# Attention weights as one exponential of a difference of logarithms, and a part of their sums as exact f32r products in three passes, in a four-layer graph network kernel

## The chip, the cores and the metric

The kernel runs on one core of a Trainium2 chip. The time is that of one execution on the device, in microseconds (us), and lower is better. Three runs of the kernel before took 836.5, 840.3 and 846.0 us. A core has several engines that run side by side, each with a queue of its own: TensorE (PE, matmuls; PEld are its weight loads), VectorE (DVE), ScalarE (ACT), GpSimd (POOL) and SyncE (SP, which issues most of the large loads).

## The reference

Four residual layers run one after the other on x (2708 nodes, 128 features) with one adjacency matrix adj (2708 x 2708). Each is followed by a layernorm. The change touches only the second, an attention layer:

```python
XW = jnp.matmul(X, W)
s_col = jnp.matmul(XW, a[0, :f])
s_row = jnp.matmul(XW, a[0, f:])
Z1 = jax.nn.leaky_relu(s_row[:, None] + s_col[None, :], negative_slope=0.01)
den = jnp.exp(Z1)
num = jnp.matmul(A, den)
att = jnp.where(num != 0, den / jnp.where(num != 0, num, 1.0), 0.0)
H = jnp.matmul(A, jnp.matmul(att, XW))
...
x = _layernorm(x + _L1_gnn_ref(x, adj, L1_gnn_W, L1_gnn_a), axis=-1)
```

Since exp(leaky(z)) is exp(0.01 z) times max(exp(0.99 z), 1), and z is a sum of a row's and a column's term, the factors exp(0.01 s) can be taken out of the large products. What stays for every pair of nodes is max(exp(0.99 (r + s)), 1), divided by num.

## The kernel before

The whole kernel is one program for one core. Most of it works on tiles of 128 partitions with up to 512 columns[...] ("psum" tiles with the tags acc0 to acc5 and twice ps). First comes layer 0 (matmuls L928), with row sums and degrees beside it. Then the nodes are sorted by one of their attention terms into GM = 24 groups of up to 126 nodes (lines 1324 to 1533). Then `grouped_attention` (line 1564) does the attention layer up to att @ XW, and `fast_rest` the rest of layer 1 and the layers 2 and 3 (the matmuls L1952, L1820, L2444, L2460).

`grouped_attention` goes over the 2708 columns in two halves of HALF = 1354, and in each over the 24 groups, so that q counts 48 groups. A half's columns are cut into chunks of 512, 512 and 330. For each q:

- `gather(q)` (L1577, on POOL) fetches the group's 126 adjacency rows from HBM three groups ahead into one of four places `gat[q]`; the first two rows of a place are free. `group_xw` (L1587) fetches the group's rows of XW.
- `numerators(q)` (line 1610) first writes max(q_b * gj_l, 1) for the group into `att` (L1618, DVE), where `q_b` and `gj_l` hold the exponentials of 0.99 times the two terms. Then for each chunk: a matmul (L1629, PE) of the group's 128 x 128 matrix with the gathered rows into a PSUM tile `num`; a copy of two rows of `num` into the first two rows of the next group's place (L1632, DVE), which carries running sums from group to group; the logarithm of `num` (L1634, ACT) into `ln_n`. Then, in the first half, the matrix of the group three ahead is made (`group_matrix`, L748, ACT; its spread of factors by a transpose on PE, L745, lies in the third chunk's tile). Last comes exp(-ln_n) over all 1354 columns (L1648, ACT). `num` tiles take turns in five buffers (`num_tags`).
- `weighted(q - 1)` (line 1650) multiplies `att` by it (L1652, DVE).
- `aggregate(q - 2)` (line 1654) adds XW's rows of the group times `att` to three sums `uacc`, one for each chunk (L1660, PE). At a half's end the sums are copied to `ut` (L1672 on ACT, L1675 on DVE).

The loop over q (line 1696) writes these out in this order, one group after the other. `queued(engine)` fixes that an engine issues the instructions within it in the order in which they are written. Beside the groups, the loop places small work: transposes of the first half's result (`node_major_u`, L1596 on PE, L1599 on ACT, in "ps" buffers) in groups 27 to 36, `tail_factors` (line 1679) at group 26, with a copy `repeated(x, ...)` (L218, DVE) in it, `added_up` (line 1550, DVE) at group 36, and `checked` (line 1559) at group 38. After the loop the remaining twelve transposes follow, among the first matmuls of the next stage.

An f32 matmul of up to 512 columns appears as two passes in the trace, with a weight load each. `sharp_products` (line 1816) in the later stages computes the same kind of product otherwise: both factors are cut into an upper part, a low part and a mix that are exact in the f32r format, and three f32r passes follow, two into a sum "upper" and one into the common sum. The two are joined at the end by a multiplication with 1 + 1/4096 and an addition. `split_rows` (line 1802) cuts the moving factor: one operation on ACT (L1806) and two on DVE (L1807, L1808).

Of the kernel before, what the change touches and what calls it, by code (L numbers as in the profile page):

```python
# [10 lines left out]
F32 = mybir.dt.float32  # L11
# [25 lines left out]
FIRST = 3  # L37
GM = 24
# [25 lines left out]


# [20 lines left out]
def kernel(  # L86
# [1225 lines left out]
    with ctx_keep:  # L1312
# [11 lines left out]
        with tc.tile_pool(name="sort", bufs=1) as st_p:  # L1324
# [54 lines left out]
            for b in range(NB):  # L1379
                w, cs = width(b), bslice(b)  # L1380
                sum_rows((3,3,2,2,1,1)[b])
                with queued(PE):
                    pr = bcast_block(rcl[:, 0, :], b, f"rb{b}")
                with queued(ACT):
                    nc.scalar.activation(q_b[:, cs], pr[:, :w], AF.Exp, scale=0.99)
# [137 lines left out]
            nc.vector.tensor_scalar(bi, e2_l, unit0[:, 1:2], None, op0=ALU.add)  # L1523
            nc.vector.tensor_copy(w_first[:, :, 0], sc[:, :FIRST])
# [39 lines left out]
    def grouped_attention(u_sb, rows_g):  # L1564
        adj_h = adjT.rearrange("k (h w) -> (k h) w", h=2)
        chunks = [(0, BW), (BW, 2 * BW), (2 * BW, HALF)]
        with tc.tile_pool(name="main", bufs=1) as mp:
            w_all = mp.tile([P, GM, P], F32, tag="w_all", name="w_all")
            xw_g = mp.tile([P, GM, F], F32, tag="xw_g", name="xw_g")
            gat, att, ln_n, uacc = {}, {}, {}, {}  # L1570
            num_tags = [("acc3", 1), ("acc4", 1), ("acc5", 1), ("ps", 2), ("ps", 2)]
# [38 lines left out]
            def numerators(q):  # L1610
# [6 lines left out]
                with queued(DVE):  # L1617
                    nc.vector.tensor_scalar(  # L1618
                        att[q], q_b[:, h0 : h0 + HALF], gj_l[:, g : g + 1], 1.0, op0=ALU.mult, op1=ALU.max
                    )  # L1620
                w = (w_first if g < FIRST else w_all)[:, g, :]
                for c, (ca, cb) in enumerate(chunks):
                    tag, nb = num_tags[(3 * q + c) % 5]
                    num = psum.tile([P, BW], F32, tag=tag, name=f"num{q}_{c}", bufs=nb)
                    if c == 2 and 0 < q and q + FIRST < GM:
                        with queued(PE):
                            group_spread_out(num[:, BW - P :], q + FIRST)
                    with queued(PE):
                        nc.tensor.matmul(num[:, : cb - ca], lhsT=w, rhs=gat[q][:, ca:cb], start=True, stop=True)  # L1629
                    if g + 1 < GM:  # L1630
                        with queued(DVE):
                            nc.vector.tensor_copy(gat[q + 1][0:2, ca:cb], num[0:2, : cb - ca])  # L1632
                    with queued(ACT):
                        nc.scalar.activation(  # L1634
                            ln_n[q][:, ca:cb],
                            num[:, : cb - ca],
                            AF.Ln,
                            scale=occ_l[:, g : g + 1],
                            bias=inval[:, g : g + 1],
                        )  # L1640
                if g + 1 == GM and not h:
                    carry(q + 1)
                if q + FIRST < GM:
                    pg = gb[:, FIRST, :] if q == 0 else num[:, BW - P :]
                    with queued(ACT):
                        group_matrix(w_all, q + FIRST, pg)
                with queued(ACT):
                    nc.scalar.activation(ln_n[q], ln_n[q], AF.Exp, scale=-1.0)  # L1648

            def weighted(q):  # L1650
                with queued(DVE):
                    nc.vector.tensor_mul(att[q], att[q], ln_n[q])  # L1652

            def aggregate(q):
# [3 lines left out]
                for c, (ca, cb) in enumerate(chunks):  # L1658
                    with queued(PE):
# [5 lines left out]
                            stop=(g == GM - 1),  # L1665
                        )
                if g == GM - 1:
                    for c, (ca, cb) in enumerate(chunks):
                        src, dst = uacc[h][c][:, : cb - ca], ut[:, h * HALF + ca : h * HALF + cb]
                        if c < 2:  # L1670
                            with queued(ACT):
                                nc.scalar.copy(dst, src)  # L1672
                        else:
# [5 lines left out]
            def tail_factors():  # L1679

                pt = ps_tile("tail_ps")
                repeated(x, NF * P)
# [13 lines left out]
            for q in range(2 * GM + 2):  # L1696
# [12 lines left out]
                if q == GM + GM // 4:  # L1709
                    with tc.issue_after(behind):  # L1710
                        fit_nodes()
                if q == GM + 2:
# [5 lines left out]
                if q == GM + GM // 2 + 2:  # L1718
# [899 lines left out]
```

## Time and profile before

| | |
|---|---|
| median of three runs | 840.3 us |
| lowest and highest | 836.5 and 846.0 us |
| the profiled execution | 836.5 us, its span 834.8 us |
| layer 0 and the row sums | 46 to 176 us of the span, PE busy 126.7 us |
| sorting into groups | 176 to 228 us, PE busy 47.9 us |
| attention, first half | 228 to 343 us, PE busy 114.4, DVE 101.9, ACT 91.6, POOL 94.7 us |
| attention, second half | 344 to 443 us, PE busy 99.0, DVE 89.2, ACT 75.2, POOL 57.5 us |
| layers 1 (rest), 2 and 3 | 457 to 835 us |

The costliest groups of the attention loop, as the page has them (line, engine, operation, output and inputs, shape, count, then busy us and mean ns of one, idle time of the engine before them and what ended it):

```profile
L1634 ACT ACTIVATE ln<-num,inval,occ_l 128x512 f32<-128x512 f32 x144 | 98.3, 725 | 46.5 <-DVE rows_g L1632 42.8
L1660 PE MATMUL uacc<-att,xw_g 128*128 128x512 f32 (+1 forms) x288 | 116.7, 542 | 0.3 <-PE num L1629 0.3
L1629 PE MATMUL num<-rows_g,w_all 128*128 128x512 f32 (+1 forms) x252 | 105.0, 543 | 0.2 <-issue 0.2
L1648 ACT ACTIVATE ln<-ln 128x1354 f32<-128x1354 f32 x48 | 64.1, 1336 | 0.9
```

How to read it: "<-" before a name of an engine says what released the waiting engine. The busy time of matmuls is modelled and their ends overlap, so PE's cadence is better read from the starts of the weight loads. A difference of 0.3 us of idle time in front of 288 matmuls says that nearly nothing is waited for there.

### The profile page before, as it was taken

What the parts mean: (1) busy time and instruction counts of PE and PEld (TensorE: products, weight loads), DVE (VectorE), ACT (ScalarE), POOL (GpSimd) and SP (SyncE); (2) the same over time, 40 slices, a digit from 0 to 9 for tenths busy, and PEclk for the clock granted to TensorE, in tenths of its full rate; (3) what the DMA queues carried; (4) which work ended last, traced back from release to release, by engine and by line L of the source; (5) the groups of instructions that cost most, each with busy time, mean ns of one, the idle gap of its engine ahead of it and who ended that gap; (6) DMA issues with size and microseconds to landing.
All of it is one profiled execution on the core that took longest, in us unless ns stands there. A gap on an engine that the chain in (4) does not pass through costs nothing.

```text
span 834.8 us, 10277 instructions
## 1 busy us (share of the span) xinstructions
PE 796.1 (95%) x3372; PEld 444.4 (53%) x3372; DVE 619.8 (74%) x1400; ACT 498.5 (60%) x887; POOL 194.9 (23%) x173
## 2 busy tenths in 40 slices
PE   4789999998999999999999999999999999999995
PEld 3345454454344555444454455564455766677774
DVE  4787645589598888889996677897588863776774
ACT  4856544214397878777776243686455665666662
POOL 5231000001388887576641000000000000000000
PEclk9799999999999999999999999999999999999997
DMA  9997559089479555445435778795985752756600
GB/s 341 366 383 274 143 34 372 28 307 382 157 258 393 179 165 172 134 121 179 150 117 176 270 266 284 238 345 190 360 288 160 239 179 69 290 188 239 226 27 16
DMA packets 94985, 181.70 MB, mean 218 GB/s; under 512 B 6272, under 2 KB 37396, under 8 KB 94584
## 3 DMA queue, kind: packets, MB, share of 16 engines
q1 hardware_dynamic: 85228, 142.62, 50.1%
q0 software_dynamic: 7680, 34.85, 13.1%
q10 hardware_dynamic: 2016, 3.49, 1.1%
q8 instruction: 29, 0.48, 0.2%
q14 instruction: 32, 0.26, 0.1%
HBM read 176.68 MB, written 4.28 MB: 217 GB/s over the span
## 4 chain that ended last, share of the span: by engine, by line
PE 83%; DVE 8%; DMA 5%; ACT 2%; issue 1%; ACTq 0%; DVEq 0%
PE a L1952 17%; PE uacc L1660 13%; PE num L1629 12%; PE a L928 11%; PE a L2460 7%; PE a L2444 6%; PE a_u L1820 5%; DMA A<-in_adjT_dram 4%; PE a L1820 2%; PE t L866 2%; DVE jk L1392 2%; PE pp L2347 1%; PE su L290 1%; PE xw L1063 1%; PE mx L2136 0%
## 5 line engine op out<-in xcount | busy, mean ns | idle before, releaser
L1634 ACT ACTIVATE ln<-num,inval,occ_l 128x512 f32<-128x512 f32 x144 | 98.3, 725 | 46.5 <-DVE rows_g L1632 42.8
L1660 PE MATMUL uacc<-att,xw_g 128*128 128x512 f32 (+1 forms) x288 | 116.7, 542 | 0.3 <-PE num L1629 0.3
L928 PE MATMUL a<-A,q_b 128*128 128x512 f32 (+2 forms) x264 | 110.8, 569 | 3.8 <-DVE q_b L963 2.6
L1577 POOL DMA_INDIRECT rows_g<-in_adjT_dram,row_i x48 | 97.3, 2028 | 62.5 <-PE num L1629 29.7
L1629 PE MATMUL num<-rows_g,w_all 128*128 128x512 f32 (+1 forms) x252 | 105.0, 543 | 0.2 <-issue 0.2
L2444 PE MATMUL a<-mask,node 128*128 128x452 f32 (+1 forms) x252 | 94.8, 458 | 0.0
L1632 DVE COPY rows_g<-num 2x512 f32<-2x512 f32 x138 | 81.2, 612 | 11.7 <-PE num L1629 7.6
L1952 PE MATMUL a<-cb,q_b 128*128 128x512 f32 (+1 forms) x222 | 89.5, 540 | 0.0
L1660 PEld LDWEIGHTS uacc<-att,xw_g 128*128 128x128 f32 x288 | 54.5, 190 | 55.1 <-issue 46.4
L2427 ACT ACTIVATE mask<-cb 128x904 fp32r<-128x904 f32 (+2 forms) x66 | 60.8, 923 | 35.0 <-PE a L2444 31.6
L1952 PE MATMUL a<-cb,xw 128*128 128x512 f32 (+1 forms) x196 | 79.4, 532 | 0.0
L1652 DVE TENSOR_TENSOR att<-att,ln 128x1354 f32<-128x1354 f32 x48 | 74.4, 1549 | 2.5 <-ACT ln L1648 2.5
L928 PEld LDWEIGHTS a<-A,q_b 128*128 128x128 f32 (+1 forms) x264 | 47.1, 196 | 53.9 <-issue 48.4
L1629 PEld LDWEIGHTS num<-rows_g,w_all 128*128 128x128 f32 x252 | 45.3, 190 | 44.8 <-issue 35.0
L2460 PE MATMUL a<-cb,edge 128*128 128x452 f32 (+1 forms) x150 | 68.9, 543 | 0.0
L1648 ACT ACTIVATE ln<-ln 128x1354 f32<-128x1354 f32 x48 | 64.1, 1336 | 0.9
L2444 PEld LDWEIGHTS a<-mask,node 128*128 128x128 f32 x252 | 46.2, 189 | 26.5 <-issue 24.1
L1219 ACT ACTIVATE xw<-A 128x2048 f32<-128x2048 f32 (+3 forms) x36 | 57.0, 1583 | 2.7 <-DMA A<-in_adjT_dram 1.8
L1587 POOL DMA_INDIRECT xw_g<-xw_d,xw_i x24 | 54.2, 2259 | 15.9 <-issue 15.6
L1952 PEld LDWEIGHTS a<-cb,q_b 128*128 128x128 f32 x222 | 38.4, 190 | 31.5 <-issue 29.4
L1618 DVE TENSOR_SCALAR att<-q_b,gj_l 128x1354 f32<-128x1354 f32 x48 | 44.4, 926 | 10.9 <-PE uacc L1660 10.9
L1806 ACT ACTIVATE a_s<-cb 128x512 fp32r<-128x512 f32 x43 | 26.6, 626 | 40.3 <-PE a L1820 29.5
(536 smaller groups left out, 1255.1 us busy)
## 6 DMA issues: line engine op xcount, KB each, us to landing
cb<-in_adjT_dram SPq DMA_DIRECT2D x10, 2816.0 KB
A<-in_adjT_dram SPq DMA_DIRECT2D x25, 1024.0 KB
cb<-in_adjT_dram SPq DMA_DIRECT2D x10, 2560.0 KB
B<-in_adjT_dram SPq DMA_DIRECT2D x18, 1024.0 KB
cb<-in_adjT_dram SPq DMA_DIRECT2D x5, 2486.0 KB
cb<-in_adjT_dram SPq DMA_DIRECT2D x5, 2260.0 KB
cb<-in_adjT_dram SPq DMA_DIRECT2D x2, 1554.0 KB
cb<-in_adjT_dram SPq DMA_DIRECT2D x1, 2464.0 KB
```

The source lines that it names most:

```text
L928: nc.tensor.matmul(acc[c][:, :w], lhsT=z[:kw, k, :], rhs=t[:kw, i, :w], start=c not in begun, stop=(d == NB - 1 and k == NT - 1), skip_gro ...
L1577: got = nc.gpsimd.indirect_dma_start(out=gat[q], out_offset=None, in_=adj_h, in_offset=bass.IndirectOffsetOnAxis(ap=row_i[:, h, g : g + 1] ...
L1629: nc.tensor.matmul(num[:, : cb - ca], lhsT=w, rhs=gat[q][:, ca:cb], start=True, stop=True)
L1632: nc.vector.tensor_copy(gat[q + 1][0:2, ca:cb], num[0:2, : cb - ca])
L1634: nc.scalar.activation(ln_n[q][:, ca:cb], num[:, : cb - ca], AF.Ln, scale=occ_l[:, g : g + 1], bias=inval[:, g : g + 1],)
L1648: nc.scalar.activation(ln_n[q], ln_n[q], AF.Exp, scale=-1.0)
L1652: nc.vector.tensor_mul(att[q], att[q], ln_n[q])
L1660: nc.tensor.matmul(uacc[h][c][:, : cb - ca], lhsT=xw_g[:, g, :], rhs=att[q][:, ca:cb], start=(g == 0), stop=(g == GM - 1),)
L1952: nc.tensor.matmul(acc()[:, :w], lhsT=weights[:, k, :], rhs=a, start=(k == 0), stop=False, skip_group_check=True)
L2427: nc.scalar.activation(mask[:, :n, :w], hold[i][0][:, t : t + n, :w], AF.Sign)
L2444: nc.tensor.matmul(acc()[:, :w], lhsT=node[:, k, j, :], rhs=mask, start=(k == 0 and j == 0 and b != 1), stop=False, skip_group_check=True,)
L2460: nc.tensor.matmul(acc()[:, :w], lhsT=edge[:, k, :], rhs=piece(k), start=(k == 0 and b == 1), stop=False, skip_group_check=True,)
```

## The change

- **One exponential.** `q_b` now holds 0.99 times the row term itself (a Copy on ACT in place of an Exp, L1385). `e1_l` and `e2_l`, once used, are filled with +0.99 and -0.99 times the group's terms. The multiplication and maximum of L1618 and the product L1652 go, and so does the exponential L1648. In their place `exponents(q)` computes max(q_b, e2_l) - ln_n in one DVE operation over 1354 columns, and `weighted(q)` takes Exp of it with the bias e1_l on ACT.
- **Order.** From the third group on (EARLY = 2), the copy of the two carried rows stands behind the chunk's logarithm instead of before it. `group_matrix` stands directly behind the third logarithm. The Exp of group q - 1 stands behind the logarithms of group q. `aggregate` takes the chunks in the order 1, 2, 0.
- **Three passes.** In the groups 3, 5, ..., 21 of each half, the first chunk (512 columns) is summed in three f32r passes, two into a new sum `upper` and one into `uacc`. `split_xw` cuts XW's rows of the group (128 columns: one operation on ACT, three on DVE), and `weighted` cuts the weights (512 columns: one on ACT, two on DVE). `upper` takes the PSUM bank acc5, so that the numerators share four buffers from the fourth group on. At a half's end one DVE operation joins `upper` to the copied sum.
- **Small work.** `repeated(x, ...)` moves from group 26 to group 24, `checked` from group 38 to group 40.

```diff
-                    nc.scalar.activation(q_b[:, cs], pr[:, :w], AF.Exp, scale=0.99)
+                    nc.scalar.activation(q_b[:, cs], pr[:, :w], AF.Copy, scale=0.99)
...
+            nc.vector.tensor_scalar(e1_l, value, 0.99, None, op0=ALU.mult)
+            nc.vector.tensor_scalar(e2_l, value, -0.99, None, op0=ALU.mult)
...
+SPLIT = (range(3,GM-2,2), range(3,GM-2,2))
...
+            first_tags = [("acc3", 1), ("acc4", 1), ("acc5", 1), ("ps", 2), ("ps", 2)]
+            num_tags = [("acc3", 1), ("acc4", 1), ("ps", 2), ("ps", 2)]
...
-                with queued(DVE):
-                    nc.vector.tensor_scalar(
-                        att[q], q_b[:, h0 : h0 + HALF], gj_l[:, g : g + 1], 1.0, op0=ALU.mult, op1=ALU.max
-                    )
...
-                    if g + 1 < GM:
+                    if q < EARLY:
                         with queued(DVE):
                             nc.vector.tensor_copy(gat[q + 1][0:2, ca:cb], num[0:2, : cb - ca])
...
+                    if EARLY <= q and g + 1 < GM:
+                        with queued(DVE):
+                            nc.vector.tensor_copy(gat[q + 1][0:2, ca:cb], num[0:2, : cb - ca])
...
+                if split(q - 1):
+                    split_xw(q - 1)
+                if q == EARLY:
+                    exponents(q - 1)
+                if q >= EARLY:
+                    exponents(q)
+
+            def exponents(q):
+                h, g = divmod(q, GM)
+                with queued(DVE):
+                    nc.vector.scalar_tensor_tensor(
+                        att[q],
+                        q_b[:, h * HALF : (h + 1) * HALF],
+                        e2_l[:, g : g + 1],
+                        ln_n[q],
+                        op0=ALU.max,
+                        op1=ALU.subtract,
+                    )
...
+            def factors(held, tag, src, w, q):
+                t = mp.tile([P, 3, w], F32R, tag=tag, name=f"{tag}{q}", bufs=2)
+                up, low, mix = held[q] = [t[:, j, :] for j in range(3)]
                 with queued(ACT):
-                    nc.scalar.activation(ln_n[q], ln_n[q], AF.Exp, scale=-1.0)
+                    nc.scalar.activation(up, src, AF.Copy, scale=UPPER)
+                with queued(DVE):
+                    nc.vector.tensor_sub(low, up.bitcast(F32), src)
+                return up.bitcast(F32), low, mix
+
+            def split_xw(q):
+                up, low, mix = factors(parts, "parts", xw_g[:, q % GM, :], F, q)
+                with queued(DVE):
+                    nc.vector.scalar_tensor_tensor(
+                        mix, up, -1.0 / LOW, low.bitcast(F32), op0=ALU.mult, op1=ALU.subtract
+                    )
+                    nc.vector.tensor_scalar(low, low.bitcast(F32), LOW, None, op0=ALU.mult)
 
             def weighted(q):
-                with queued(DVE):
-                    nc.vector.tensor_mul(att[q], att[q], ln_n[q])
+                g = q % GM
+                if q < EARLY - 1:
+                    exponents(q)
+                with queued(ACT):
+                    nc.scalar.activation(att[q], att[q], AF.Exp, bias=e1_l[:, g : g + 1])
+                if split(q):
+                    a = att[q][:, :BW]
+                    up, low, mix = factors(rows3, "split", a, BW, q)
+                    with queued(DVE):
+                        nc.vector.scalar_tensor_tensor(mix, low.bitcast(F32), LOW + 1.0, a, op0=ALU.mult, op1=ALU.add)
...
-                for c, (ca, cb) in enumerate(chunks):
+                for c in (1, 2, 0):
+                    ca, cb = chunks[c]
+                    if split(q) and not c:
+                        if h not in upper:
+                            upper[h] = acc_tile(5, f"upper{h}")
+                        for j in range(3):
+                            with queued(PE):
+                                nc.tensor.matmul(
+                                    uacc[h][0] if j == 2 else upper[h],
+                                    lhsT=parts[q][j],
+                                    rhs=rows3[q][j],
...
+                            if not c:
+                                with queued(DVE):
+                                    nc.vector.scalar_tensor_tensor(
+                                        dst, upper[h], 1.0 + 1.0 / LOW, dst, op0=ALU.mult, op1=ALU.add
+                                    )
```

## The prediction

> **What bounds the kernel now.** I read the busy shares first, then the chain of waits, then one table of windows, then single groups in the timeline. TensorE (PE) is busy 95% of the span, and the chain lies on it for 83%:
>
> ```profile
> PE 796.1 (95%) x3372; PEld 444.4 (53%) x3372; DVE 619.8 (74%) x1400; ACT 498.5 (60%) x887; POOL 194.9 (23%) x173
> ...
> PE 83%; DVE 8%; DMA 5%; ACT 2%; issue 1%; ACTq 0%; DVEq 0%
> ```
>
> The change lies in the attention loop, which runs from 228 to 450 us. The table of windows (window, us, then busy us of PE, weight loads, DVE, ACT, POOL) for three steady stretches of it:
>
> ```profile
> 264.00:318.00 54.00, 54.00 (x153) 27.19 (x152) 49.00 (x60) 43.05 (x60) 46.88 (x24) 1.00 0.63 200
> 346.00:396.00 50.00, 50.00 (x140) 24.82 (x139) 45.08 (x60) 39.26 (x54) 35.69 (x25) 1.00 0.46 144
> 400.00:440.00 40.00, 40.00 (x108) 20.05 (x108) 35.88 (x47) 29.45 (x35) 19.32 (x7) 1.00 0.39 122
> ```
>
> PE never stops, at a granted clock of 1.00; DVE is at about 90%, ACT at 74 to 80%. So only PE work removed here shortens the stage, and DVE is the next bound, 10% behind. One group in the timeline (start us, us; DVE, then ACT):
>
> ```profile
> 405.13 0.93 DVE L1618 TENSOR_SCALAR att<-q_b,gj_l 128x1354 f32<-128x1354 f32 x1 [0.26 <-PE uacc L1660]
> 405.99 0.68 DVE L1632 COPY rows_g<-num 2x512 f32<-2x512 f32 x1
> 406.85 1.09 DVE L1632 COPY rows_g<-num 2x512 f32<-2x512 f32 x2 [0.18 <-PE num L1629]
> 407.87 1.55 DVE L1652 TENSOR_TENSOR att<-att,ln 128x1354 f32<-128x1354 f32 x1
> ...
> 406.70 2.15 ACT L1634 ACTIVATE ln<-num,inval,occ_l 128x512 f32<-128x512 f32 x3 [1.02 <-DVE rows_g L1632]
> 408.89 1.33 ACT L1648 ACTIVATE ln<-ln 128x1354 f32<-128x1354 f32 x1
> ```
>
> What to see: DVE is through with a group shortly before the next begins. The period is 4.55 us (DVE's 405.13 to 409.68); a group with a transpose or a spread of the group's factors beside it takes 4.66. ACT's first logarithm starts only when DVE's carry copy of the same PSUM tile has ended.
>
> **What the Trainium skill says.** "PSUM — Partial Sum Buffer", section "PSUM bank collisions raise a hardware error": two engines may not touch one bank at once, reads included. The trace agrees: the 42.8 us of ACT's waits for L1632, two readers of one tile. "VectorE: DVE Perf Modes", section "The perf-mode tier table": fp32 with one SBUF source runs at 2x, with two sources at 1x. Agrees: 0.93 us (L1618) against 1.55 us (L1652) for 1354 columns. "ScalarE: Activation LUTs", section "Step-by-step: what each stage is for": a bias costs no instruction of its own, so the new Exp takes the old one's time.
>
> **The price of the split.** Weight loads mark PE's cadence (start us, us):
>
> ```profile
> 480.21 0.19 PEld L1820 LDWEIGHTS a_u<-a_s,u_split 128*128 128x128 f32 x1 [0.24 <-issue]
> 480.64 0.19 PEld L1820 LDWEIGHTS a_u<-a_s,u_split 128*128 128x128 f32 x1 [0.24 <-issue]
> 480.87 0.19 PEld L1820 LDWEIGHTS a<-a_s,u_split 128*128 128x128 f32 x1
> 481.10 0.42 PEld L1952 LDWEIGHTS a<-cb,xw 128*128 128x128 f32 x2
> 481.76 0.19 PEld L1952 LDWEIGHTS a<-cb,xw 128*128 128x128 f32 x1 [0.24 <-issue]
> ```
>
> A load goes out as the pass before begins. f32 passes of 512 columns stand 0.43 us apart, f32r passes 0.23. An f32 product is two passes, 0.86 us; three f32r passes take 0.69. Gain 0.17 us. With 10 split groups in each half: 20 x 0.17 = **-3.4 us**. Lower bound 0 (DVE or ACT sets the pace and hides it). Upper: 512 columns at 2.4 GHz plus 2.5 ns are 216 ns by "TensorE: Matmul & The Clock Gate", section "Wait — 56ns, not 53.3ns?", an estimate: 3 x 0.216 = 0.65, gain 0.21, 4.3 us in all; the loads here (0.19 us plus a gap) speak for 0.23.
>
> **Does DVE still fit?** It loses L1618 and L1652 and gets one two-source operation of 1354 columns, by L1652 1.55 us. Back to back, in DVE's run at 263.71 to 267.63 us, a group costs 1.48 + 0.83 + 1.61 = 3.92. After: 1.61 + 1.48 = 3.1. A split group adds three small dependent operations on 128 columns (0.29, 0.29 and 0.2 by L1787, L1788 and L1758: 0.75) and two on 512 columns (0.69 each by L1807 and L1808: 1.37). A pair of groups: 8.3 us, against PE's 2 x 4.66 - 0.17 = 9.14, or 8.93 without transposes.
> ACT for a pair in the first half: 2 x (2.0 Ln + 0.46 matrix + 1.33 Exp) + 0.63 (L1806) + 0.3 (128 columns) = 8.5. It fits too.
> From the third group on, the carry copy stands behind Ln in the program order (before, Ln stood behind the copy). What is queued behind a waiting copy on DVE is the group's other copies, the xw parts, the exponents and the split; the next group's numerators on PE wait for the copy, the Exp on ACT one group later for the exponents. Numerators now share four PSUM buffers instead of five; each was read at least a group earlier. Walk of a split group from PE's start at 0: Ln 1.06 to 3.2, matrix 3.66, upper xw 3.95, Exp 5.3, upper weights 5.9; DVE: copies 1.85 to 3.85, xw parts 4.85, exponents 6.4, two split operations 7.8. The next group's copies then run 7.8 to 9.6, the first done at 8.5; PE wants it at 9.17, so 0.6 us is left. The split product reads its last part at 8.5 + 0.45, over 1 us after 7.8. No steady stall: **0**, both ends below.
>
> **The edges.**
> - Start. Before, PE's first sum starts at 233.40. Now weights wait for Ln, then DVE, then ACT behind the next group's logarithms: by the same walk the first Exp ends at 234.0 and the sum starts at 234.1; the second waits for the exponents of group 1, which stand behind group 2's copies on DVE, until 239.6 instead of 238.13. +1.5, of which 0.3 is absorbed where PE waited anyway (254.54 to 254.71 and a like gap at 257, behind a late gather): **+1.2** (0 to 2).
> - Middle. Before, PE idles from 342.96 to 344.08 for DVE's L218. That copy is issued two groups earlier now, but the small tail product sits in a "ps" buffer which the second numerator needs, and its DVE reader is queued behind the ACT copy (0.59), the new join of the upper sum (0.75) and a copy (0.5). About 1.2 us again: **+0.1** (-1.0 to +0.7).
> - In the second half DVE's six operations of L1550 (0.9 us in all; two of PE's groups there took 0.2 us longer) fall into a split group, and transposes share two "ps" buffers: **+0.5** (0 to 1.5).
> - End. The last but one Exp stands behind the last logarithms: +0.25. The join adds ACT 0.59 and DVE 0.75 ahead of the transposes, 1.7 us with handovers; two products of the next stage (1.72 us) now stand before them in PE's order and cover it, and the stall of 0.68 us at 452.5 (DVE behind POOL's memset) shrinks. **-0.3** (-0.6 to +1.7, the cover gone).
> - At nothing: Exp to Copy in q_b (0.6 us either way), two 24-column DVE operations before the loop (DVE idles 5.6 us there, behind PE's row sums), the moved gps product (tiny). Gathers and POOL's queue keep their order; POOL was 47 of 54 us busy, and the groups get only 2% shorter. SP's loads are not moved.
>
> Sum: -3.4 + 1.2 + 0.1 + 0.5 - 0.3 = **-1.9 us**. The profiled run took 836.5 (span 834.8), so 834.6. It is the lowest of the three runs; their median is 840.3, so I forecast 840.3 - 1.9 = **838.4**.
>
> **Rivals.**
> 1. DVE's chain becomes the pace (slower). Place: the even groups, where copies, parts, exponents and split stand in one queue with three handovers to ACT. For it: 8.3 of 8.93 us. Against it: 0.6 us of slack in the walk. It decides once waits exceed 0.7 us a pair. If DVE waits out Exp and the upper part (1.5 us more), a pair takes 9.8 against 9.31 before: 20 x 0.5 = +10, 850 us. Chance 0.10.
> 2. The edges cost nothing and the middle gap closes: -4.3 - 1.0 - 0.6 = -5.9, 834.4. For it: the tail's operand is ready earlier. Against: the "ps" buffer. Chance 0.20.
> 3. The passes don't run at the quick rate, three at 0.43: +8.6 instead of -3.4, 850 us; L1820 speaks against it, in the same form. Chance 0.03.
> The forecast itself has 0.67.
>
> **Numbers.** Within 1% (8.4 us) a measurement of this kernel can hardly tell a change from none: its three runs span 836.5 to 846.0. Forecast and rival 2 both lie within it; rivals 1 and 3 give 0.13 near +1.1%, of which scatter takes some back: slower 0.11. All that PE can lose in this stage is some 7 us, so faster by over 1% needs scatter too: 0.12; same 0.77. The forecast's bounds are about -6 to +4, with the scatter of a median of some 3 us: 832 to 845 leaves out rivals 1 and 3 and a little on either side.
>
> **What would show it.** Right: PE busy in all of 264 to 318, f32r loads 0.23 us apart there, pairs of 9.1 us, DVE near 90%, a PE gap near the first two sums and near 343. Wrong: PE waits on DVE's copies or on the split parts in every second group (rival 1), no gap at 343 (rival 2), or f32r passes at another cadence.

## The result, and the profile after

The changed kernel takes 835.5 us (median of 15 executions, 833.2 to 840.3), the kernel before 843.4 us beside it (15 executions, 836.5 to 847.7). The ratio is 0.9924, with a 95% interval from 0.9897 to 0.995: by the means 6.4 us less (the medians lie 7.9 us apart), where 1.9 us had been forecast. In a later series of executions (experiment 10 below) it was 0.9932. Ratios and their intervals leave out executions more than 1.5% above the fastest of their kernel; the medians and ranges given here include them. The profiled execution of the changed kernel took 837.1 us, its span 835.2 us, which is no shorter than the 834.8 us of the profiled kernel before. So the spans alone would say "no change", and two things must be taken apart: where the change acts, and how each kernel varies from one execution to the next.

First the page of the changed kernel: busy shares, the chain that ended last by engine, and the groups that answer to those shown of before (the fetches of the loop's rows on POOL are added).

```profile
PE 794.5 (95%) x3392; PEld 448.5 (54%) x3392; DVE 620.3 (74%) x1456; ACT 518.2 (62%) x927; POOL 136.8 (16%) x173
...
PE 82%; DVE 9%; DMA 5%; ACT 3%; issue 1%; ACTq 0%; DVEq 0%
...
L1637 ACT ACTIVATE ln<-num,inval,occ_l 128x512 f32<-128x512 f32 x144 | 99.1, 725 | 21.8 <-PE num L1632 18.2
L1632 PE MATMUL num<-rows_g,w_all 128*128 128x512 f32 (+1 forms) x252 | 104.5, 542 | 0.0
L1725 PE MATMUL uacc<-att,xw_g 128*128 128x512 f32 (+1 forms) x248 | 99.8, 535 | 2.1 <-issue 1.2
...
L1697 ACT ACTIVATE att<-att,e_l 128x1354 f32<-128x1354 f32 x48 | 68.2, 1421 | 2.5 <-issue 2.1
...
L1583 POOL DMA_INDIRECT rows_g<-in_adjT_dram,row_i x48 | 49.6, 1034 | 116.9 <-PE num L1632 85.3
```

What to see: ScalarE's logarithms no longer wait 42.8 us for the copies, since they come first. And POOL, which had been counted at nothing: 194.9 us busy before, 136.8 after, at the same 173 instructions. The page of before has the same fetches at twice the time each:

```profile
L1577 POOL DMA_INDIRECT rows_g<-in_adjT_dram,row_i x48 | 97.3, 2028 | 62.5 <-PE num L1629 29.7
```

The three stretches of the table of windows (columns as in the prediction):

```profile
264.00:318.00 54.00, 54.00 (x161) 28.57 (x160) 50.29 (x77) 48.98 (x72) 34.31 (x24) 1.00 0.63 206
346.00:396.00 50.00, 49.21 (x143) 25.56 (x142) 43.61 (x72) 43.43 (x66) 20.01 (x25) 1.00 0.46 151
400.00:440.00 40.00, 40.00 (x116) 21.21 (x115) 37.80 (x59) 33.35 (x44) 7.04 (x7) 1.00 0.40 122
```

TensorE never stops in the first and the third; in the second it has one gap of 0.79 us, shown below. In the first, DVE is at 93% (before 91%), ACT at 91% (80%), POOL at 64% (87%). The split itself, in the chain of waits of the second half (start, us, what):

```profile
435.65 1.41 PE uacc L1725 x4
437.06 0.46 PE upper L1715 x2
437.52 0.23 PE uacc L1715
437.76 2.27 PE num L1632 x6
440.03 2.27 PE uacc L1725 x6
442.30 2.28 PE num L1632 x6
444.58 1.41 PE uacc L1725 x4
```

Three f32r passes take 0.69 us, and a pair of groups 444.58 - 435.65 = 8.93 us, to the digit what the sum had. The edges, in TensorE's timeline:

```profile
237.09 2.51 PE L1725 MATMUL uacc<-att,xw_g 128*128 128x512 f32 x6 [1.24 <-issue]
...
347.43 1.68 PE L1632 MATMUL num<-rows_g,w_first 128*128 128x512 f32 x4 [0.79 <-DVE e_tail L1754]
```

The first line is the later first sum; the second is the gap at the halves' boundary, behind the tail's operand in a "ps" buffer. The kernel before has a gap of the same length there, behind the copy L218:

```profile
343.73 0.35 PE L1683 MATMUL tail_ps<-w1ext,x 128*128 128x1 f32 x2 [0.79 <-DVE x L218]
```

**Where the time lies.** To compare kernels without what happens elsewhere I take one length from each profile: from the first numerator matmul (225.50 us before, 228.54 after) to a run of eight matmuls in the next stage that all versions have (L1952 before, L2025 after; 471.07 and 471.37 us). I call it the loop's length:

| profile | loop's length, us | span, us |
|---|---|---|
| before, the profile of the prediction | 245.57 | 834.8 |
| changed kernel | 242.83 | 835.2 |

So the loop is 2.74 us shorter. The span isn't, because the sorting ahead of it ended 3.0 us later in this execution. That start varied from 224.6 to 229.2 us over all profiles of this study. It isn't a part of the change: its mean is 227.0 us in the six profiles with the exponents of before and 227.1 in the eight with the new ones. The granted clock from 176 to 228 us doesn't order these starts either: it was 0.93 in the profile that began the loop at 224.6 us (experiment 5) and in this one, with 228.5. But 2.74 is not 6.4. What of the rest?

### The profile page after: what moved, and what is told of

It reads as the page before. It is cut to its first block, busy times and chain, and to the rows that moved or that the text cites. A ratio compares the mean times of both kernels' runs of the same rounds, so it can differ in the third digit from the quotient of the medians.

```text
span 835.2 us, 10312 instructions
## 1 busy us (share of the span) xinstructions
PE 794.5 (95%) x3392; PEld 448.5 (54%) x3392; DVE 620.3 (74%) x1456; ACT 518.2 (62%) x927; POOL 136.8 (16%) x173
## 4 chain that ended last, share of the span: by engine, by line
PE 82%; DVE 9%; DMA 5%; ACT 3%; issue 1%; ACTq 0%; DVEq 0%
PE a L2025 17%; PE num L1632 12%; PE uacc L1725 11%; PE a L931 11%; PE a L2533 7%; PE a L2517 6%; PE a_u L1893 5%; DMA A<-in_adjT_dram 4%; PE a L1893 2%; PE t L869 2%; DVE jk L1395 2%; PE upper L1715 1%; PE pp L2420 1%; ACT ln L1637 1%; PE list L1485 1%
## 5 line engine op out<-in xcount | busy, mean ns | idle before, releaser
L1632 PE MATMUL num<-rows_g,w_all 128*128 128x512 f32 (+1 forms) x252 | 104.5, 542 | 0.0
L1725 PE MATMUL uacc<-att,xw_g 128*128 128x512 f32 (+1 forms) x248 | 99.8, 535 | 2.1 <-issue 1.2
L1650 DVE COPY rows_g<-num 2x512 f32<-2x512 f32 x132 | 76.9, 611 | 17.8 <-ACT ln L1637 14.7
L2025 PE MATMUL a<-cb,q_b 128*128 128x512 f32 (+1 forms) x222 | 89.5, 540 | 0.0
L2025 PE MATMUL a<-cb,xw 128*128 128x512 f32 (+1 forms) x196 | 79.6, 532 | 0.0
L1663 DVE SCALAR_TENSOR_TENSOR att<-q_b,e_l,ln 128x1354 f32<-128x1354 f32 x48 | 77.5, 1615 | 0.3 <-ACT ln L1637 0.3
L931 PEld LDWEIGHTS a<-A,q_b 128*128 128x128 f32 (+1 forms) x264 | 47.1, 196 | 54.2 <-issue 48.6
L1632 PEld LDWEIGHTS num<-rows_g,w_all 128*128 128x128 f32 x252 | 45.5, 190 | 48.9 <-issue 37.7
L1697 ACT ACTIVATE att<-att,e_l 128x1354 f32<-128x1354 f32 x48 | 68.2, 1421 | 2.5 <-issue 2.1
L1583 POOL DMA_INDIRECT rows_g<-in_adjT_dram,row_i x48 | 49.6, 1034 | 116.9 <-PE num L1632 85.3
L1725 PEld LDWEIGHTS uacc<-att,xw_g 128*128 128x128 f32 x248 | 46.8, 190 | 39.6 <-issue 24.9
L2025 PEld LDWEIGHTS a<-cb,q_b 128*128 128x128 f32 x222 | 38.4, 190 | 31.6 <-issue 29.4
L1249 DVE TENSOR_TENSOR ut<-ut,A 128x2048 f32<-128x2048 f32 (+3 forms) x24 | 43.8, 1824 | 8.9 <-DMA A<-in_adjT_dram 7.9
L1593 POOL DMA_INDIRECT xw_g<-xw_d,xw_i x24 | 43.0, 1792 | 18.8 <-PE gb_first L748 11.8
```

Source lines behind the costliest of these rows:

```text
L931: nc.tensor.matmul(acc[c][:, :w], lhsT=z[:kw, k, :], rhs=t[:kw, i, :w], start=c not in begun, stop=(d == NB - 1 and k == NT - 1), skip_gro ...
L1663: nc.vector.scalar_tensor_tensor(att[q], q_b[:, h * HALF : (h + 1) * HALF], e2_l[:, g : g + 1], ln_n[q], op0=ALU.max, op1=ALU.subtract,)
L1697: nc.scalar.activation(att[q], att[q], AF.Exp, bias=e1_l[:, g : g + 1])
L1725: nc.tensor.matmul(uacc[h][c][:, : cb - ca], lhsT=xw_g[:, g, :], rhs=att[q][:, ca:cb], start=(g == 0), stop=(g == GM - 1), skip_group_chec ...
L2025: nc.tensor.matmul(acc()[:, :w], lhsT=weights[:, k, :], rhs=a, start=(k == 0), stop=False, skip_group_check=True)
```

## The experiments

**1 and 2. The kernel before, profiled again.** The edit is none. The profile of the prediction was that of the fastest of all fifteen executions above, so the first question is what a usual one looks like.

> The kernel before, unchanged, for a second profile: its profiled execution was the fastest of fifteen (836.5 us against a median of 843.4), so it cannot show what most executions pay. Theory A1 (port): DVE's L1618 holds the port that POOL needs, gathers come late in most executions, and the loop from 225 to 450 us is longer here by several us, with DVE's carry copies waiting for the DMA and PE idle. Theory A2 (clock): the loop keeps its length within 1 us, and the time lies in the sorting stage from 200 to 225 us, at a lower granted clock.

> The kernel before once more, a third profile. As for the second: A1 puts the difference to 834.8 us of span into the loop (PE idle behind late gathers), A2 into the sorting stage at a lower granted clock. If both profiles are near 837 us, neither is shown.

Measured: 847.2 us (span 845.5) and 849.9 us (span 848.2), with loops of 253.83 and 255.84 us. The 37 executions of the kernel before that were taken beside these two run from 836.5 to 851.0. In these two profiles the chain of waits inside the loop doesn't lie on TensorE throughout. The first of them, start, us, what:

```profile
308.94 3.09 POOL rows_g L1577
312.03 0.96 issue
312.99 3.61 POOL xw_g L1587
316.60 0.15 issue
316.75 0.02 POOLq L1577
316.77 0.14 issue
316.91 4.35 POOL rows_g L1577
...
333.35 8.79 DMA rows_g<-in_adjT_dram,row_i
```

GpSimd issues one gather after the other with only some 0.3 us between, TensorE waits for DVE's copies, and these wait for the gathered rows. The waits of L1632 for them (us in all, number), in the profile of the prediction, in this one and in the other:

```profile
  DMA rows_g<-in_adjT_dram,row_i: 3.6, 3
...
  DMA rows_g<-in_adjT_dram,row_i: 15.5, 7
...
  DMA rows_g<-in_adjT_dram,row_i: 22.6, 9
```

In both profiles of the changed kernel no copy waits for rows. TensorE is busy 109.7 and 107.3 us of the 116 between 228 and 344 us, against 114.7. The granted clock there is 0.99 or more, so the clock isn't it.

Why GpSimd is that slow shows in the timeline of the prediction's own profile (start, us, engine):

```profile
290.26 3.10 POOL L1587 DMA_INDIRECT xw_g<-xw_d,xw_i  x1 [0.30 <-issue]
...
290.46 1.55 DVE L1652 TENSOR_TENSOR att<-att,ln 128x1354 f32<-128x1354 f32 x1
...
292.31 0.93 DVE L1618 TENSOR_SCALAR att<-q_b,gj_l 128x1354 f32<-128x1354 f32 x1 [0.31 <-PE uacc L1660]
...
293.66 0.94 POOL L1577 DMA_INDIRECT rows_g<-in_adjT_dram,row_i  x1 [0.30 <-issue]
```

A gather alone takes 0.94 us; one beside L1652 and L1618 takes 3.10 us and ends 0.12 us after L1618 does. With 0.30 us between gathers, a group costs GpSimd 0.94 + 3.10 + 2 x 0.30 = 4.64 us. TensorE's group takes 4.66. So GpSimd was full even in the best execution: 46.88 us busy and 24 x 0.30 us between, 54.1 of the 54 us of the window. It kept up only as long as one gather of two met no operation of DVE.

**3. The change without the split.** This separates the three passes from the rest.

```diff
-SPLIT = (range(3,GM-2,2), range(3,GM-2,2))
+SPLIT = ((), ())
```

> The change without the three passes (no split groups, no join), everything else kept, four buffers for the numerators as well. By the sum of the prediction the split is worth 3.4 us: two groups take 9.31 us instead of 9.15, and the time is about 3 us above that of the change, a ratio to before of 0.996. If the gain of 0.76% is the exponential's and the order's alone, the ratio stays at 0.992.

Measured: ratio 0.9975 (0.9958 to 0.9992), median 839.3 us, 835.5 to 842.4 in 22 executions. Its loop is 245.17 us long: 0.4 us less than that of before at its best, 2.34 us more than that of the changed kernel. The gathers of rows take 0.94 us in the median, and those of XW's rows stand beside the one remaining long operation:

```profile
277.70 0.94 POOL L1583 DMA_INDIRECT rows_g<-in_adjT_dram,row_i  x1 [1.03 <-PE num L1632]
...
278.89 1.61 DVE L1663 SCALAR_TENSOR_TENSOR att<-q_b,e_l,ln 128x1354 f32<-128x1354 f32 x1
278.94 2.38 POOL L1593 DMA_INDIRECT xw_g<-xw_d,xw_i  x1 [0.30 <-issue]
```

GpSimd now waits for TensorE (1.03 us a group) instead of the other way round: 39.0 + 24 x 0.30 = 46.2 us of 54. What follows: the split is worth 2.3 us of the loop (the two ratios, from different series of executions, lie 0.5% apart), and the rest of the change, whose arithmetic on TensorE is the same as before, takes the executions above 843 us away.

**4. The old first operation put back, into a tile that nobody reads.** Experiment 3 plus a needless copy of L1618 in each group.

```diff
+                idle = mp.tile([P, HALF], F32, tag="idle", name=f"idle{q}", bufs=2)
+                with queued(DVE):
+                    nc.vector.tensor_scalar(
+                        idle, q_b[:, h0 : h0 + HALF], gj_l[:, g : g + 1], 1.0, op0=ALU.mult, op1=ALU.max
+                    )
```

> As the one without split, but DVE's first operation of each group as it was before (0.93 us, one source, 1354 columns) is issued again, into a tile that nobody reads. DVE then has 3.1 + 0.83 us a group, within PE's 4.66, so its own time is covered. A1 (port): POOL's gathers go back from about 1.0 to 2.0 us each, and the time rises by some 4 us over the one without the operation, with a wider spread. A2 (clock) or no effect: within 1.5 us of it.

Measured: 846.4 us (844.1 to 854.0), ratio 1.0074 (1.0045 to 1.0102); loop 252.38 us. GpSimd is busy 47.89 us of the window with 21 gathers, so 54.2 of 54, and the chain lies on it and on its transfers from 238 to 292 us; the copies wait for gathered rows for 13.5 us in 9 waits (none in experiment 3). One operation of 0.93 us, on an engine that then is 81% busy in the window, costs 7 us through another engine's queue.

**7. Another kind of operation of the same length.** My theory at this point named the kind: one f32 source at the double rate. So the needless operation gets two tensor sources and 780 columns, 1.01 us (the edit against experiment 4).

```diff
-                    nc.vector.tensor_scalar(
-                        idle, q_b[:, h0 : h0 + HALF], gj_l[:, g : g + 1], 1.0, op0=ALU.mult, op1=ALU.max
-                    )
+                    nc.vector.scalar_tensor_tensor(
+                        idle[:, :780], q_b[:, h0 : h0 + 780], gj_l[:, g : g + 1],
+                        q_b[:, h0 + 500 : h0 + 1280], op0=ALU.max, op1=ALU.subtract,
+                    )
```

> The changed kernel without the split, with a needless operation on VectorE in each group as in the run before it, of about the same duration (0.93 us), but with two tensor sources (780 columns) instead of one (1354 columns). If what holds up GpSimd is the kind of VectorE's operation (one f32 source at the double rate), GpSimd's gathers stay at a median of about 1 us and the time at that of the version without the split, 839 us (838 to 841). If it is VectorE's time or its load, gathers at 3 us and 846 us, as with the one-source operation.

Measured: 844.2 us (836.9 to 853.5), ratio 1.0054 (1.0025 to 1.0084), loop 253.28 us, not the 839 us that the theory asked for. The median gather of rows is 0.945 us, but the mean 1.755: of a group's two gathers one is held, and the other often too. So the kind isn't what decides, and that part of the theory falls. The timeline shows the hold by two-source operations:

```profile
247.09 3.76 POOL L1583 DMA_INDIRECT rows_g<-in_adjT_dram,row_i  x1
...
247.48 1.61 DVE L1673 SCALAR_TENSOR_TENSOR att<-q_b,e_l,ln 128x1354 f32<-128x1354 f32 x1
...
249.01 1.01 DVE L1625 SCALAR_TENSOR_TENSOR idle<-q_b,gj_l 128x780 f32<-128x780 f32 x1
```

The gather ends at 250.85, 0.83 us after the second operation. "VectorE's load" isn't the other answer either: the changed kernel has more of it in the same window (50.29 us busy against 44.33) and gathers of rows of 1.03 us in the mean.

**9. The first operation moved between two copies (kernel before).** If it is the uninterrupted run of such operations that holds a gather, breaking the run should help.

```diff
-                with queued(DVE):
-                    nc.vector.tensor_scalar(
-                        att[q], q_b[:, h0 : h0 + HALF], gj_l[:, g : g + 1], 1.0, op0=ALU.mult, op1=ALU.max
-                    )
...
                             nc.vector.tensor_copy(gat[q + 1][0:2, ca:cb], num[0:2, : cb - ca])
+                    if c == 0:
+                        with queued(DVE):
+                            nc.vector.tensor_scalar(
+                                att[q], q_b[:, h0 : h0 + HALF], gj_l[:, g : g + 1], 1.0, op0=ALU.mult, op1=ALU.max
+                            )
```

> The kernel before with its first operation of a group (L1618) placed between the group's first and second carry copy, so that it no longer stands directly behind the product L1652. Nothing is computed otherwise. In the traces so far a gather on GpSimd ends about 0.83 us after the last of the VectorE operations on SBUF tensors that it ran beside, and isn't held by copies from PSUM. If the uninterrupted run of such operations is what makes GpSimd's queue the bound, it falls from 2.48 us to 1.55 us: the held gathers take 2.4 us or less instead of 3.1, GpSimd is busy 40 us or less of 54 (in a stretch like 264 to 318 us) instead of 47, and the time is 837 us with a narrow spread (835 to 842). If GpSimd's load follows VectorE's busy time, or gathers are late for another reason, the time stays at that of the kernel before, with its spread of over 10 us.

Measured: 855.2 us (852.0 to 868.1), ratio 1.0145 (1.0107 to 1.0182), loop 270.06 us in the profile. Neither expectation came true: it got worse. The window:

```profile
264.00:318.00 54.00, 48.68 (x125) 22.09 (x126) 39.65 (x50) 36.01 (x50) 48.54 (x18) 0.97 0.51 170
```

GpSimd is full again (48.54 + 18 x 0.30 = 53.9), and the chain of waits lies on it and on its transfers from the loop's start to 291 us, with fewer instructions done: the gathers of rows take 3.0 us in the median. The gap of about 0.9 us that two copies leave between L1618 and L1652 is too short for a gather to be through, so a gather can be held by both. The full queue is confirmed as what sets the time; that a shorter run of operations would empty it is refuted.

**12. One gather fewer (kernel before).** The last experiment changes no instruction of DVE, ACT or TensorE and takes work from GpSimd, with the transfers that belong to it. The rows of XW come unsorted in one load ahead of the loop, so the sums are taken with other rows than the layer's.

```diff
+            with tc.issue_after(behind):
+                nc.sync.dma_start(
+                    out=xw_g[:, 3:, :], in_=xw_d[: 21 * P, :].rearrange("(t p) f -> p t f", p=P)
+                )
...
-                    if q + 3 < GM:
-                        group_xw(q + 3, behind)
```

> The kernel before, with nothing changed on VectorE, ScalarE or TensorE; the 21 gathers of XW's rows inside the first half's loop are left out, and one plain load ahead of the loop fills their places with rows of XW in unsorted order (so the sums are taken with other rows, in the same time). GpSimd then issues one gather a group. If GpSimd's full queue is what makes the kernel before slow and scattered, the time is 836.5 us or less, and its spread at most 7 us (before: over 10); GpSimd is busy under 35 us of 54 in 264 to 318 us, TensorE busy throughout. If late rows come from the memory traffic or from VectorE's own load, the time and its spread stay those of the kernel before (841 us).

Measured: 836.7 us, 834.8 to 838.0 in 22 executions, beside 837.2 us, 835.0 to 847.5 in 27 executions, of the kernel before; ratio 0.9975 (0.9958 to 0.9992); loop 244.91 us.

```profile
264.00:318.00 54.00, 54.00 (x152) 27.04 (x151) 48.27 (x58) 41.88 (x59) 36.14 (x12) 1.00 0.49 161
```

The remaining gathers are still held (median 3.08 us; GpSimd is busy 36.1 us where under 35 had been expected), no copy waits for rows any more, and the long executions are gone: 11 of the 27 of before took over 838.0 us, none of these 22. The median is only 0.5 us lower, since the kernel before took 837.2 us beside it, not the 841 us of the expectation. Less is moved, too (161 instead of 200 GB/s in the window), but experiment 4 fills the queue with an operation that adds no transfer. So GpSimd's full queue was what spread the times of before. Seven versions with a measured spread, from several series of executions, with how full GpSimd is in the window from 264 to 318 us (busy time plus 0.30 us for each instruction):

| version | GpSimd, us of 54 | executions, us | loop in profiles, us |
|---|---|---|---|
| 12, before with one gather a group | 39.7 | 834.8 to 838.0 | 244.91 |
| changed kernel | 41.5 | 833.2 to 840.3 | 242.83, 242.84 |
| 3, without the split | 46.2 | 835.5 to 842.4 | 245.17 |
| before | 54.1, 54.2 | 835.0 to 851.0 | 245.57, 253.83, 255.84 |
| 4, first operation back | 54.2 | 844.1 to 854.0 | 252.38 |
| 7, two-source operation | 54.2 | 836.9 to 853.5 | 253.28 |
| 9, first operation between copies | 53.9 | 852.0 to 868.1 | 270.06 |

**6. The split alone, in the kernel before.** Old exponents, old order of copies and logarithms; the split as in the changed kernel, with its order of chunks and its four buffers for the numerators, `split_xw` in `weighted`.

```diff
 def weighted(q):
     with queued(DVE):
         nc.vector.tensor_mul(att[q], att[q], ln_n[q])
+    if split(q):
+        split_xw(q)
+        a = att[q][:, :BW]
+        up, low, mix = factors(rows3, "split", a, BW, q)
```

> The kernel before with the three passes alone: old exponents (a maximum, an exponential, a product), old order of copies and logarithms, four numerator buffers. By the sums of durations VectorE needs 2 x 3.92 + 2.12 = 9.96 us for a pair of groups and TensorE 9.14: if VectorE then sets the pace, a pair takes 10 us instead of 9.31, about 20 x 0.65 = 13 us slower than before, TensorE with idle time in every split pair behind VectorE. If VectorE's work for the split hides in its slack, 3.4 us faster than before.

Measured: 880.2 us (879.0 to 882.3), ratio 1.0471 (1.0405 to 1.0538), three times the loss that was expected. In the timeline the split's last operation (L1682) starts at 292.76 and again at 304.15 us: 11.39 us a pair, not 10. DVE isn't full (46.92 us of 54). In the chain of waits there, copies, logarithms, exponential and the split's parts follow one another, DVE and ACT by turns. GpSimd, at 34.30 us, isn't the cause here.

**8. The changed kernel with the copies first.** Only the order of a copy and its logarithm is taken back.

```diff
-                    if q < EARLY:
+                    if g + 1 < GM:
                         with queued(DVE):
                             nc.vector.tensor_copy(gat[q + 1][0:2, ca:cb], num[0:2, : cb - ca])
...
-                    if EARLY <= q and g + 1 < GM:
-                        with queued(DVE):
-                            nc.vector.tensor_copy(gat[q + 1][0:2, ca:cb], num[0:2, : cb - ca])
```

> The changed kernel with the old order of each chunk: the copy of two carried rows ahead of its logarithm in all groups. If the new order only moves waits that nobody feels, the same time as the changed kernel within 0.2% (835.5), ScalarE waiting some 40 us for the copies again. If it is what lets the split fit (ScalarE has 8.5 us of work in a pair of 9.14), TensorE waits for split parts or exponents in the first half's pairs: 0.3 to 0.6 us a pair, 3 to 6 us slower than the changed kernel.

Measured: 871.8 us (870.8 to 873.9), ratio 1.0365 (1.0315 to 1.0415), loop 281.60 us: 38.8 us more than the changed kernel, where 3 to 6 had been expected. The timeline of DVE and ACT shows a closed ring:

```profile
294.89 0.69 DVE L1699 SCALAR_TENSOR_TENSOR split<-split,att 128x512 fp32r<-128x512 f32 x1
...
295.50 1.68 DVE L1635 COPY rows_g<-num 2x512 f32<-2x512 f32 x3
...
296.21 1.97 ACT L1637 ACTIVATE ln<-num,inval,occ_l 128x512 f32<-128x512 f32 x3 [2.43 <-DVE rows_g L1635]
...
298.21 1.63 DVE L1660 SCALAR_TENSOR_TENSOR att<-q_b,e_l,ln 128x1354 f32<-128x1354 f32 x1 [1.03 <-ACT ln L1637]
...
299.76 1.68 DVE L1635 COPY rows_g<-num 2x512 f32<-2x512 f32 x3
...
300.47 1.97 ACT L1637 ACTIVATE ln<-num,inval,occ_l 128x512 f32<-128x512 f32 x3 [0.63 <-DVE rows_g L1635]
...
303.80 1.62 DVE L1660 SCALAR_TENSOR_TENSOR att<-q_b,e_l,ln 128x1354 f32<-128x1354 f32 x1
...
304.32 0.63 ACT L1676 ACTIVATE split<-att 128x512 fp32r<-128x512 f32 x1
```

Copy, logarithms, exponents, the next copy, its logarithms, the Exp, the split: each waits for the one before, DVE and ACT by turns, and the ring takes 11.17 us a pair (294.89 to 306.06, the next start of L1699) while DVE is busy 76% of the window from 264 to 318 us and TensorE waits. (The view of the chain lays this stretch on GpSimd and on time without a visible wait; but GpSimd is busy 22.4 of the 54 us, and idle for 2.75 to 3.18 us before each gather of rows, behind TensorE.) With the logarithm ahead of the copy, it depends on TensorE alone, and the ring is open. So the order is no small thing beside the split: without it the changed kernel is slower than the kernel before. A sum of durations by engine can't show such a ring; a walk along the dependencies can.

**5, 10 and 11. Two edges mended.** The changed kernel with the exponents of group 1 right behind those of group 0, and `tail_factors` at group 44 instead of 26; once alone, then beside the changed kernel in one series.

```diff
-                if q == EARLY:
-                    exponents(q - 1)
...
-                if q < EARLY - 1:
-                    exponents(q)
+                if q == 0:
+                    exponents(0)
+                    exponents(1)
...
-                if q == GM + 2:
+                if q == GM + 20:
                     with queued(PE, DVE, ACT):
                         tail_factors()
```

> The changed kernel with two edges mended: the exponents of group 1 are issued right behind those of group 0 instead of two groups later, and tail_factors stands at group 44 instead of 26. If the start and the half's boundary cost what their gaps in the profile show (0.95 us later start of the second sum, a PE gap of 0.79 us at the boundary), about 1.7 us less than the changed kernel: some 833.8 beside 835.5, PE without a gap at the boundary. If other work only takes the gap's place (the numerators wait for the copies or a gather instead), no difference from the changed kernel within 0.2%.

> The changed kernel itself, on the same chip as the version with the two edges mended: 835.5 us, spread 833 to 841. Its gathers should not be late in any profile, and the loop's length, from the first numerator to the next stage, within 0.3 us of that in the first profile.

> The changed kernel with the two edges mended, beside the changed kernel on one chip: if the gaps were all that it mends, 1.7 us less than that (0.2%). If the 832.3 us of the first run of it held something else too, some 3 us less.

Measured: 832.3 us (830.4 to 834.4), ratio 0.9896 (0.9848 to 0.9944), and in the second series 833.9 us (833.3 to 835.1), ratio 0.9909 (0.9877 to 0.9941), beside 836.2 us (834.9 to 838.2), ratio 0.9932 (0.9906 to 0.9957), of the changed kernel, which repeats as expected. The loops are 240.74 and 240.75 us against 242.83 and 242.84: 2.09 us less, to the hundredth alike in both profiles, where 1.7 was expected. At the boundary TensorE goes on without a gap:

```profile
343.93 2.44 PE L1632 MATMUL num<-rows_g,w_first 128*128 128x512 f32 x6
...
346.20 2.44 PE L1724 MATMUL uacc<-att,xw_g 128*128 128x512 f32 x6
```

The first run's larger lead (3.2 us to the changed kernel's first median) was taken in two series, and its profile began the loop at 224.61 us, the earliest of all; it isn't counted. The ratios' intervals overlap; it is the two medians of one series (2.4 us apart, with ranges that meet only between 834.9 and 835.1) and the loops that show the gain.

## Why the prediction was right in direction and too small

To set the sum of the prediction against the loop, here are five stretches of it, between starts on TensorE in the chain of waits: the first numerator, the sums of the groups q = 5, 22, 24 and 44, and the run of eight matmuls in the next stage (before 225.50, 257.33, 336.12, 346.46, 439.18, 471.07 us; changed kernel 228.54, 261.50, 338.74, 349.11, 440.03, 471.37 us).

| stretch | before | after | measured | forecast |
|---|---|---|---|---|
| start, with one split group | 31.83 | 32.96 | +1.13 | +1.2 - 0.17 |
| first half, nine split groups | 78.79 | 77.24 | -1.55 | -1.53 |
| boundary | 10.34 | 10.37 | +0.03 | +0.1 |
| second half, nine split groups | 92.72 | 90.92 | -1.80 | +0.5 - 1.53 |
| end, with one split group | 31.89 | 31.34 | -0.55 | -0.3 - 0.17 |
| the loop | 245.57 | 242.83 | -2.74 | -1.9 |

- **What bounds.** TensorE is the bound in the loop, before and after, wherever the gathers come in time. Right.
- **The split, -3.4.** The passes run at 0.23 us, a pair takes 9.14 to 9.15 us in the first half (starts in the chain at 254.46, 263.61 and 272.75 us) and 8.93 in the second. Right. In the loop 2.3 us of it are left beside experiment 3. There the boundary costs 0.7 us less (9.68 instead of 10.37 us, and no gap), without the join; the remaining 0.4 us stay open.
- **DVE's slack of 0.6 us.** No stall in any steady pair. Right. The new Exp takes 1.42 us, not the old one's 1.34 as the prediction had it; at ACT's 91% that cost nothing.
- **Start, +1.2.** The first sum begins 8.55 us after the first numerator instead of 7.90, the second 14.22 instead of 12.63, so +1.6; by the sixth sum 0.3 of it are absorbed, and +1.3 are left. Right, with the mechanism.
- **Middle, +0.1.** 0.0, with a gap of 0.79 us before and after, and behind the "ps" buffer as forecast. Right. (The 1.12 us that the prediction gave for before hold the tail's small product, 0.35 us, too.)
- **Second half, +0.5.** Wrong in sign: -0.3. Two groups of numerators that took 2.63 instead of 2.44 us before (at 367.31 and 390.79 us) no longer do, and no new loss came. This term makes up nearly all of the 0.8 us between -1.9 and -2.74.
- **End, -0.3.** -0.4. Right.
- **The rivals.** The first, DVE as the pace, didn't come; it was priced too low, as far as experiments 6 and 8 show, which lose the slack in another way: by their ratios they are 40 and 31 us slower than before, not 10. The second, "the edges cost nothing", has with -5.9 the number nearest to the 6.4 measured, but by luck: the edges cost what was forecast. The third fails by the 0.23 us.
- **The step that failed**, for what lies beyond the loop at its best, is one costed at nothing: "Gathers and POOL's queue keep their order; POOL was 47 of 54 us busy, and the groups get only 2% shorter." The order is kept, but not the length: each gather is held by DVE's operations, and the change takes one of these away. Busy time was read as load, without the 0.30 us between gathers; with them POOL had nothing left. And the profile was of the fastest execution, in which a full queue still keeps up. The forecast put the scatter of before (836.5 to 846.0) on the measurement; much of it was in the kernel. Experiments 1, 2, 4 and 12 show it: loops from 245.6 to 255.8 us before, 242.8 twice after. That the forecast time, 838.4 us, comes within 3 us of the measured 835.5 is in part luck: it started from 840.3 us, and the kernel before then took 843.4.

"SBUF — State Buffer", section "Who interferes with whom", of the Trainium skill would have pointed to it: VectorE and GpSimd share a pair of ports, and a VectorE operation in a two-port mode, or with two SBUF inputs where GpSimd reads SBUF, takes it for the whole instruction. The trace agrees: 0.94 us alone, 3.10 us beside L1652 and L1618. Two-source operations hold a gather as well (2.38 us beside L1663). The section also infers that a `tensor_tensor` leaves the issue of a DMA alone; that doesn't hold here, as the last section shows (2.78 us).

**Open:** how much of the 6.4 us comes from late gathers can't be told from profiles of single executions; 2.7 us lie between the loops at their best, and that the rest is the late gathers' share fits the scatter, but no run adds it up. Nor is the 6.4 a fixed size: the medians of the kernel before were 843.4, 841.2, 837.4, 841.2 and 837.2 us in five series, and the changed kernel was measured only beside the first and the fourth. Why the full queue costs more in some series than in others wasn't looked into. Why a gather that starts 0.4 to 1 us ahead of the long operation, beside copies from PSUM (experiment 7, 247.09), doesn't get through either, wasn't tried. Nor was the order of copies and logarithms without the split.

## What to carry to other kernels

Add the gaps between a queue's instructions to its busy time before calling it free, and look at more than the fastest execution: a kernel whose times spread wider than its neighbours' may have a full queue that keeps up only by luck. Count what an operation does to the engine that shares a port with it, not only to its own. And before work is put into the slack of two engines that feed each other, follow the ring of dependencies once around; its length, not the sum of each engine's work, is the price.

## What the runs showed of the hardware

- A gather of 126 rows costs GpSimd 0.94 us alone. Held, it ended 0.12 us after a one-source operation (L1618) and 0.82 to 0.83 us after a two-source one (L1663, and L1625 of experiment 7). A product of two tensors holds it in the same way, in experiment 6 to 302.10 us, 0.82 us after the product's end:

```profile
299.32 2.78 POOL L1590 DMA_INDIRECT xw_g<-xw_d,xw_i  x1 [0.30 <-issue]
...
299.73 1.55 DVE L1676 TENSOR_TENSOR att<-att,ln 128x1354 f32<-128x1354 f32 x1
```

  That fits a gather with two moments that need the port, one near its start and one near its end, but it wasn't tested.
- Breaking up a run of such operations with short copies between them (experiment 9) made the gathers no shorter (3.0 us in the median) and the kernel 1.5% slower.
- The loop's length repeats to 0.01 us in two executions where GpSimd isn't full (242.83 and 242.84, 240.74 and 240.75 us), and differs by 10 us where it is (245.57 to 255.84).
